# A two-layer decoder on one core: layer 0's first units in another order and its norm pinned behind the exps; in layer 1's joint attention the scaling one step later, copies bound to an engine, norms and routing in smaller pieces

## The chip, the cores and the metric

The kernel runs on one core of a Trainium2 chip. The metric is the device time of one launch in microseconds; it is compared by medians of several runs on the same chip. Beside the times there is one execution recorded by the hardware profiler. Engines are named as in the profile: PE is TensorE (matmuls and transposes; PEld its weight loads), DVE is VectorE, ACT is ScalarE, POOL is GpSimd, SP is the engine that only issues DMAs.

## The reference, cut to what matters

Input x has 8 batches of 512 tokens of 256 numbers, the context 64 tokens per batch. Everything is float32. `norm` is a layer norm without weights.

```python
# layer 0
x = norm(x + decay_attention(x))    # 16 heads of 16: softmax((q k^T / 16) * exp(-0.01 |i-j|)) v, k and v from a latent of 64
x = norm(x + cross_attention(x, context, mask))
x = norm(x + butterfly_ffn(x))      # its weight products are built on the chip, on POOL, during decay_attention
# layer 1
x = norm(x + causal_attention(x))   # 16 heads of 64, rotary positions
x = norm(x + joint_attention(x, context))   # 8 heads of 64; keys are 512 tokens + 64 of the context
xn = layernorm(x) * gamma + beta    # experts: top 2 of 8
p  = softmax(xn @ router.T / 1.5);  w, idx = top_k(p, 2)
x = norm(2 * x + sum over the 2 experts of w * (silu(xn @ W1[e]) @ W2[e]))
```

The residual counts twice (the expert layer adds it and the decoder adds it again), which is why the kernel doubles x before it stores it as the start of the sum.

## The kernel before

The kernel is recorded as one program; a scheduler places each engine's instructions by the order in which they were recorded and by its own estimate of when their operands are there. Inside `tc.manual_schedule(engines={PE})` PE keeps the recorded order exactly; an instruction given to `tc.keep_in_program_order` keeps its place among the others of its engine. PSUM tiles come from three pools, "s" (scores), "t" (transposes) and "o" (products); a tile of a pool can only be written again when its last reader is done. `evac` copies a PSUM tile to SBUF, in turn on DVE (L108) and ACT (L110).

**Layer 0's self attention.** A unit is a batch b and a group g of four heads; there are 32. Per unit, four `l0_maxima` compute scores of 128 queries against all keys (s_sc, L423), and a fused DVE operation multiplies by the decay and takes the row maximum (scored, L428); DVE then subtracts it on the diagonal block (diag, L438). `l0_shift` works the maximum into q and has POOL make four products (kr, kf, qf, qr, L459), so that the transposed scores can be computed directly: `l0_probs(b, g, kt)` for one block kt of 128 keys writes two tiles s_st (L472, L475, and the diagonal block by a transpose, L477), and ACT turns each into pt by an exp (L481). `l0_values` multiplies by v (L492). A step of the loop is (b, g, kt): probabilities of this unit, values of the step before, maxima of the unit two later, then a piece of work for other batches (`later`: transposes and projections of batch b+1, output product of batch b-1). The last piece of the output calls `normed(..., on_act=True)`: DVE adds the residual (L541) and takes statistics (L213, L214, ve L215), POOL raises to the power -1/2 (rs, L216), DVE makes the bias (ve, L218) and ACT scales (x<-r,ve,rs, L221). POOL's remaining time in this stage goes to the butterfly's weights (L299).

Ahead of the loop both first units are projected, all their 8 maxima computed, the first shifted, and the third projected. PE's order in layer 0 is the scheduler's.

**Layer 1's joint attention.** A step is (b, c, i): a pair of heads c, a block i of 128 queries; 128 steps. `_pipeline` runs, for step s, the scores of s (s_sc, L1106; DVE takes nm, L1110; ACT the exp, L1111; DVE the reciprocal of the sums, L900, and two scalings p<-p,rsum, L902), the transposes of step s-2 (tP2 L1123, tP L1128, evacuated by `evac`), the values of s-6 (o_pv, L1140 and L1148), a piece of projection for the next pair (`l1x_ahead`: t_qk L1060, t_v L1073), and one piece of the list `put_off`. That list gets, when a batch's values are done, its output product in two pieces (o_out, L239; the second ends with the norm), and then the routing: `route_norm` (z = norm of x, x doubled at L1196 and stored by SP), `route_transposes` (tZ, L1206, two PSUM tiles, copied by ACT with gamma and beta), `route_odds` (o_r, L1221, softmax), `route_picks` (the two largest; the token's number is copied into z, L1259), `route_places` (o_rank, ranks, and eight indirect DMAs from POOL that write rows of z to DRAM, L1283). z has a single buffer, so the next batch's writes into it wait for these DMAs. PE keeps the recorded order here.

**The experts** run over tiles of 128 or 256 routed rows: SP loads xr and the weights (L1406 to L1408), PE transposes and multiplies (L1418, L1440, L1457). The last batch's routing pieces are taken one per expert step from `last_route`.

Of the kernel before, what the change touches and what calls it, by code (L numbers as in the profile page):

```python
# [49 lines left out]
def decoder_kernel(ctx: ExitStack, tc: tile.TileContext, a: dict, out: bass.AP):  # L50
# [154 lines left out]

    def normed(dst, r, on_act=False):
# [9 lines left out]
        pool.tensor_tensor(rs, ve, mhalf, ALU.pow)  # L216
        if on_act:
            dve.scalar_tensor_tensor(ve, mv[:, :, 0], -1.0, rs, ALU.mult, ALU.mult)  # L218
        for i in range(NT):
            if on_act:  # L220
                act.activation(dst[:, i, :], r[:, i, :], AF.Identity, bias=ve[:, i : i + 1], scale=rs[:, i : i + 1])  # L221
                continue
            dve.tensor_scalar(
                dst[:, i, :], r[:, i, :], mv[:, i, 0:1], rs[:, i : i + 1], ALU.subtract, ALU.mult
            )

    def r_tile():
        return work.tile([P, NT, D], F32, tag="r", name="r", bufs=1)

    def project_and_norm(b, lhs, w, n, plus, later=None):  # L230

        r = r_tile()

        def piece(i2):
            o = u_tile("o_out").rearrange("p (i n) -> p i n", i=2)
            for j in range(2):
                i = 2 * i2 + j
                for c in range(n):
                    pe.matmul(  # L239
                        o[:, j, :],  # L240
                        lhsT=lhs[:, c, i * P : (i + 1) * P],
                        rhs=w[:, c, :],
                        start=(c == 0),
                        stop=(c == n - 1),
                    )
            dve.tensor_tensor(r[:, 2 * i2 : 2 * i2 + 2, :], o, plus[:, 2 * i2 : 2 * i2 + 2, :], ALU.add)
            if i2 == NT // 2 - 1:
                normed(xs[b], r)
# [214 lines left out]
    def l0_probs(b, g, kt):  # L463
# [15 lines left out]
        for s in s2:  # L479
            pt = ph.tile([P, 2, S], F32, tag="pt", name="pt", bufs=3)  # L480
            act.activation(pt, s, AF.Exp, scale=1.0 / 16.0)  # L481
            pts.append(pt)
# [39 lines left out]
    def l0_output(b):  # L522
# [10 lines left out]
        def product(i2):  # L533
# [8 lines left out]
            if i2 == 1:  # L542
                normed(xs[b], r, on_act=True)

        return [partial(turn, 0), partial(turn, 1), partial(product, 0), partial(product, 1)]

    with tc.tile_pool(name="bfly", bufs=1, side="right") as bfly, phase("l0_self") as ph, psum("a", 3, 1, 1):
# [8 lines left out]
        diags = [slot(f"diag{i}").rearrange("p (i h n) -> p i h n", i=NT, h=4) for i in range(2)]  # L556
        dve.tensor_tensor(wkT, wkT, wvT, ALU.add)
        o = o_tile("o_wlat")
        for c in range(KC):
            for k in range(KC):  # L560
                pe.matmul(
                    o[:, c * 64 : (c + 1) * 64],
                    lhsT=wkT[:, k, c * P : (c + 1) * P],
                    rhs=wdown[:, k, :],
                    start=(k == 0),
                    stop=(k == KC - 1),
                )
        dve.tensor_copy(wlat.rearrange("p c n -> p (c n)"), o[:, 0 : KC * 64])
# [4 lines left out]
        later = []  # L573
        for piece in l0_prepare(0):
            piece()
        for u in units[:2]:
            l0_project(*u)
        for u in units[:2]:
            for i in range(NT):
                l0_maxima(*u, i)  # L580
            if u == units[0]:
                l0_shift(*u)
        l0_project(*units[2])
        for n, (b, g) in enumerate(units):
            ahead2 = units[n + 2] if n + 2 < len(units) else None
            if g == 0 and b + 1 < NB:
                later.extend(l0_prepare(b + 1))
            for kt in range(NT):
# [4 lines left out]
                elif n:  # L593
                    l0_values(*units[n - 1], NT - 1)
                if ahead2:
                    l0_maxima(*ahead2, kt)

                if kt == 1:
                    if n + 1 < len(units):
                        l0_shift(*units[n + 1])  # L600
                elif kt == 2:
# [14 lines left out]
        for piece in later:  # L616
            piece()
        for _ in butterfly:
            pass
# [284 lines left out]
    put_off = []  # L904

    def groups(stage):

# [53 lines left out]
    def out_done(b, c, o, w, n, plus, then=None):  # L961
# [4 lines left out]
        if c == n - 1:  # L966
            project_and_norm(b, aT, w, n, plus(), put_off)
            if then:
                then(b)
# [126 lines left out]
    def l1x_scores(b, c, i):  # L1096
# [12 lines left out]
        for j, s in enumerate(ss):  # L1109
            dve.tensor_reduce(nm[:, j : j + 1], s, AX.XY, ALU.max, negate=True)  # L1110
            act.activation(  # L1111
                p[:, j, :].rearrange("p (t n) -> p t n", t=2), s, AF.Exp, bias=nm[:, j : j + 1], accum_out=sums[:, j : j + 1]
            )
        scaled(p, sums, S + S2)
        live["p", b, c, i] = p

    def l1x_transposes(b, c, i):
        p = live.pop(("p", b, c, i)).rearrange("p j n -> p (j n)")
        if i == 0:
# [3 lines left out]
        pe.transpose(t, p[:, S : S + P], ident)  # L1123
        evac(pt2[:, i * P : (i + 1) * P], t)
        for j in range(2):
            t = t_tile("tP")
            for k in range(NT):
                pe.transpose(t[:, k, :], p[:, (S + P) * j + k * P : (S + P) * j + (k + 1) * P], ident)  # L1128
            evac(pt[j][:, :, i * P : (i + 1) * P], t)

# [58 lines left out]
    def over_i(c):  # L1189
        return c.unsqueeze(1).to_broadcast([P, NT, NE])  # L1190

    def route_norm(b):
# [5 lines left out]
        live["z", b] = z  # L1198

# [37 lines left out]
    def greatest(pick, left):  # L1237
# [7 lines left out]
        return pick  # L1245

    def route_picks(b):
        pr = live.pop(("pr", b))
        rest = e_tile("rest")
        picks = [greatest(e_tile("pick0"), pr)]  # L1250
        dve.scalar_tensor_tensor(rest, picks[0], -2.0, pr, ALU.mult, ALU.add)
# [369 lines left out]
```

## Time and profile before

| | |
|---|---|
| median of 3 runs | 3543.11 us (3541.12 to 3548.39) |
| the profiled execution | 3548.88 us, its span 3547.2 us, mean granted clock of PE 0.965 |
| busy in the span: PE, DVE, ACT, POOL | 3332.7, 2082.5, 1510.1, 1115.3 us |

By stage, from the profile's windows:

| stage, us of the span | length | PE busy | DVE busy | ACT busy | POOL busy | PE clock |
|---|---|---|---|---|---|---|
| 0 to 62, loads and first units | 62 | 49.25 | 30.16 | 7.44 | 16.64 | 0.81 |
| 100 to 800, layer 0's self attention | 700 | 655.17 | 488.67 | 312.10 | 532.75 | 0.96 |
| 850 to 1260, cross attention and butterfly | 410 | 390.15 | 256.41 | 150.81 | 70.53 | 0.95 |
| 1260 to 2175, layer 1's causal attention | 915 | 882.19 | 645.10 | 518.64 | 224.22 | 0.99 |
| 2175 to 2985, joint attention | 810 | 757.38 | 535.29 | 340.88 | 100.75 | 0.97 |
| 2985 to 3502, experts | 517 | 513.08 | 70.01 | 120.57 | 115.69 | 1.00 |

A line such as `PE s_sc L423 <- ACT pt L481: 23.2, 6, 3.9` says that PE's instruction on line 423 stood idle for 23.2 us in total, 6 times, at most 3.9 us, until ACT's instruction on line 481 was done. In a timeline the columns are start, duration, engine, line, operation, output<-inputs, shapes and count; in square brackets is the engine's idle time ahead of it, and what ended that. A row of the windows has the stretch and its length, then for each of PE, PEld, DVE, ACT and POOL the busy time, then PE's granted clock, the DMA engines' share and GB/s.

### The profile page before, as it was taken

The numbers are of one execution on the slowest core, as the hardware profiler recorded it, in microseconds if no ns is written. First come the engines' busy times: TensorE is split into PE (matmuls) and PEld (weight loads), VectorE is DVE, ScalarE is ACT, GpSimd is POOL, SyncE is SP. The second block draws the span as 40 slices with busy tenths as digits, with TensorE's granted clock in tenths as the row PEclk, the third lists the DMA queues.
The fourth block names the chain that finished last, engine by engine and source line by source line (L and its number), as shares of the span: only waits on it lengthen the run. The fifth ranks groups of instructions, "written<-read, shape, count | busy, mean of one in ns | idle before, by whom it ended". The sixth has DMA issues, their size and how long they took to land. (4 is left out here: it accounts for less than half of the span.)

```text
span 3547.2 us, 52530 instructions
## 1 busy us (share of the span) xinstructions
PE 3332.7 (94%) x19574; PEld 2092.0 (59%) x19574; DVE 2082.5 (59%) x5710; ACT 1510.1 (43%) x3139; POOL 1115.3 (31%) x1032
## 2 busy tenths in 40 slices
PE   8989999998999989999999999999999998999995
PEld 3333434345666656666666666555555555888884
DVE  5777766675666556777777775666666665211012
ACT  2444444443443335655556654444444433222222
POOL 3868677772221122222222220011111111222222
PEclk8999999999999999999999999999999999999997
DMA  4100011111000079422333330000000004666674
GB/s 132 31 19 25 22 37 37 36 36 47 5 2 1 1 195 259 77 37 38 38 40 43 40 52 4 4 19 19 22 16 14 17 13 143 206 185 187 183 230 139
DMA packets 166001, 234.96 MB, mean 66 GB/s; under 512 B 26569, under 2 KB 128649, under 8 KB 165746
## 3 DMA queue, kind: packets, MB, share of 16 engines
q1 hardware_dynamic: 139010, 175.83, 15.8%
q0 software_dynamic: 25584, 51.57, 10.2%
q10 hardware_dynamic: 1152, 4.19, 0.3%
q8 instruction: 156, 2.56, 0.3%
q14 instruction: 99, 0.81, 0.1%
HBM read 135.83 MB, written 61.11 MB: 56 GB/s over the span
## 5 line engine op out<-in xcount | busy, mean ns | idle before, releaser
L428 DVE CUSTOM_DVE_ANT_0 scored<-s_sc,decay 128x512 f32<-128x512 f32 x512 | 323.5, 687 | 223.9 <-PE s_sc L423 222.7
L281 ACT ACTIVATE p<-p,nm 128x128 f32<-128x128 f32 (+3 forms) x512 | 282.5, 553 | 301.7 <-DVE nm L270 300.4
L865 POOL DMA_DIRECT2D qk<-turned x256 | 208.2, 1232 | 593.4 <-issue 304.6
L481 ACT ACTIVATE pt<-s_st 128x1024 f32<-128x1024 f32 x256 | 261.1, 1023 | 268.2 <-PE s_st L477 237.9
L902 DVE TENSOR_SCALAR p<-p,rsum 128x576 f32<-128x576 f32 (+4 forms) x768 | 300.3, 433 | 10.0
L1111 ACT ACTIVATE p<-s_sc,nm 128x576 f32<-128x576 f32 x256 | 189.6, 743 | 221.7 <-DVE nm L1110 200.8
L1477 DVE TENSOR_SCALAR y<-o_y,share 128x256 f32<-128x256 f32 x71 | 34.2, 483 | 408.9 <-PE o_y L1457 408.9
L1440 PE MATMUL s_h<-xnT,we 128*128 128x256 f32 (+1 forms) x1248 | 260.3, 362 | 0.0
L270 DVE CUSTOM_DVE_ANT_0 p<-s_sc,tabs 128x128 f32<-128x128 f32 (+3 forms) x512 | 225.1, 484 | 57.4 <-PE s_sc L925 57.3
L1457 PE MATMUL o_y<-we,h 128*128 128x256 f32 x1136 | 251.4, 379 | 0.0
L1457 PEld LDWEIGHTS o_y<-we,h 128*128 128x128 f32 x1136 | 215.3, 190 | 29.0
L1478 POOL DMA_INDIRECT total<-y,to x71 | 110.2, 1552 | 388.4 <-DVE y L1477 219.8
L1440 PEld LDWEIGHTS s_h<-xnT,we 128*128 128x128 f32 x1248 | 216.7, 191 | 24.3 <-ACT xnT L1419 0.2
L1110 DVE TENSOR_REDUCE nm<-s_sc 128x1 f32<-128x576 f32 x256 | 183.3, 748 | 72.7 <-PE s_sc L1106 71.7
L423 PE MATMUL s_sc<-k,q 32*128 32x512 f32 x1024 | 175.6, 674 | 25.8 <-ACT pt L481 23.2
L110 ACT COPY pt<-tP 128x512 f32<-128x512 f32 (+1 forms) x224 | 109.9, 491 | 208.5 <-PE tP L1123 117.7
L958 ACT COPY pt<-tP 128x384 f32<-128x384 f32 (+1 forms) x384 | 173.0, 514 | 45.3 <-PE tP L957 44.8
L925 PE MATMUL s_sc<-qk 64*128 64x128 f32 (+3 forms) x1024 | 176.8, 461 | 13.7 <-DMA qk<-turned 10.3
L1106 PE MATMUL s_sc<-k,q 64*128 64x288 f32 x1024 | 169.4, 440 | 7.7 <-ACT p L1111 7.5
L957 PE MATMUL tP<-ident,p 128*128 128x128 f32 x1280 | 169.5, 276 | 5.3 <-ACT pt L958 4.0
L957 PEld LDWEIGHTS tP<-ident,p 128*128 128x128 f32 x1280 | 144.9, 141 | 49.4 <-issue 28.0
L981 PE MATMUL o_pv<-pt,vc 128*64 128x128 f32 (+1 forms) x2304 | 167.5, 290 | 0.0
(280 smaller groups left out, 6474.0 us busy)
## 6 DMA issues: line engine op xcount, KB each, us to landing
we<-in_mo_w SPq DMA_DIRECT2D x78, 1024.0 KB, 5.5
rows_in<-zero SPq DMA_DIRECT2D x64, 530.0 KB, 13.2
qk<-turned POOLq DMA_DIRECT2D x256, 128.0 KB, 4.5
coef<-in_ff_upw SPq DMA_DIRECT2D x40, 256.0 KB, 3.3
coef<-in_ff_dnw SPq DMA_DIRECT2D x40, 256.0 KB, 3.2
xr<-rows_in SPq DMA_DIRECT2D x32, 265.0 KB, 5.7
x<-in_x SPq DMA_DIRECT2D x8, 512.0 KB, 9.9
total<-x SPq DMA_DIRECT2D x8, 512.0 KB, 2.9
```

What stands on the lines that cost most here:

```text
L270: dve.tensor_tensor_reduce(out=p[:, j, 0:n], in0=s[:, j, 0:n], in1=m, scale=-scale, scalar=3.0e38, op0=ALU.add, op1=ALU.min, accum_out=nm[ ...
L281: act.activation(p[:, j, 0:n], p[:, j, 0:n], AF.Exp, bias=nm[:, j : j + 1], scale=-1.0, accum_out=sums[:, at + j : at + j + 1],)
L428: dve.tensor_tensor_reduce(out=scored[:, h, :], in0=s[:, j, :], in1=decay[:, i, :], scale=1.0, scalar=-3.0e38, op0=ALU.mult, op1=ALU.max, ...
L481: act.activation(pt, s, AF.Exp, scale=1.0 / 16.0)
L865: pool.dma_start(out=qk[h : h + 32], in_=other[g : g + 32], accum_op=ALU.add)
L902: dve.tensor_scalar(p[:, j, 0:n], p[:, j, 0:n], rsum[:, j : j + 1], None, ALU.mult)
L925: pe.matmul(s[:, j, at : at + n], lhsT=q[h : h + 64, i * P : (i + 1) * P], rhs=k[h : h + 64, 0:n], start=True, stop=True,)
L957: pe.transpose(t[:, n, :], p[:, j, at * P : (at + 1) * P], ident)
L1110: dve.tensor_reduce(nm[:, j : j + 1], s, AX.XY, ALU.max, negate=True)
L1111: act.activation(p[:, j, :].rearrange("p (t n) -> p t n", t=2), s, AF.Exp, bias=nm[:, j : j + 1], accum_out=sums[:, j : j + 1])
L1440: pe.matmul(s[:, j, :], lhsT=w1[:, c, f * P : (f + 1) * P], rhs=xnT[:, c, :], start=(c == 0), stop=(c == KC - 1),)
L1457: pe.matmul(o, lhsT=h[:, f, i * P : (i + 1) * P], rhs=w2[:, f, :], start=(f == 0), stop=(f == 7),)
```

## The change

In layer 0:

- `normed` can hand its scaling back in a list (`then`) instead of recording it at once. Layer 0's output norm does so, and the main loop records the scaling at kt = 1, after that step's exps; the scalings and the exps are kept in program order on ACT.
- The start is written out in PE's own order: both transposes of x, then o_wlat, o_lat, the projection of unit 0, its maxima with the values' product and the projection of unit 1 between them, the shift, the projection of unit 2, and only two of unit 1's four maxima. The other two are taken in unit 0's steps, whose maxima go 2, 2, 1, 1.

In layer 1's joint attention:

- `l1x_scaled` (reciprocal and two scalings) is a stage of its own, recorded one step after its scores.
- The tP2 tile is always copied by ACT, tP's first by ACT and its second by DVE.
- The norms are taken apart: the output's norm statistics come with the second product, x's scaling one step later; z's statistics one step later, its scaling another one later; the doubling of x is moved to the step of tZ; the choice of experts is three pieces (`route_pick`, `route_picks`, `route_places`). The list is so 3 steps longer for most batches; for batch 6 two pairs of pieces are put together, and its list is one step longer than before. `last_route` has no empty pieces now.

```diff
-        for i in range(NT):
+        def scaling(held=lambda instruction: instruction):
             if on_act:
...
+        if then is None:
+            scaling()
+        else:
+            then.append(scaling)
...
-            act.activation(pt, s, AF.Exp, scale=1.0 / 16.0)
+            tc.keep_in_program_order(act.activation(pt, s, AF.Exp, scale=1.0 / 16.0))
...
-                normed(xs[b], r, on_act=True)
+                normed(xs[b], r, on_act=True, then=scalings)
...
-        for piece in l0_prepare(0):
-            piece()
-        for u in units[:2]:
-            l0_project(*u)
-        for u in units[:2]:
+        with tc.manual_schedule(engines={PE}):
+            turn0, turn1, latent, values = l0_prepare(0)
+            turn0()
+            turn1()
...
+            latent()
+            l0_project(*units[0])
+
+            between = [values, partial(l0_project, *units[1])]
             for i in range(NT):
-                l0_maxima(*u, i)
-            if u == units[0]:
-                l0_shift(*u)
-        l0_project(*units[2])
+                l0_maxima(*units[0], i)
+                if between:
+                    between.pop(0)()
+            l0_shift(*units[0])
+            l0_project(*units[2])
+
+            for i in range(2):
+                l0_maxima(*units[1], i)
         for n, (b, g) in enumerate(units):
-            ahead2 = units[n + 2] if n + 2 < len(units) else None
+
+            maxima = [(*units[n + 2], i) for i in range(NT)] if n + 2 < len(units) else []
+            if n == 0:
+                maxima = [(*units[1], i) for i in range(2, NT)] + maxima
...
-                if ahead2:
-                    l0_maxima(*ahead2, kt)
-
+                for _ in range(-(-len(maxima) // (NT - kt))):
+                    l0_maxima(*maxima.pop(0))
+
+                if kt == 1 and n + 1 < len(units):
+                    l0_shift(*units[n + 1])
                 if kt == 1:
-                    if n + 1 < len(units):
-                        l0_shift(*units[n + 1])
+
+                    if scalings:
+                        scalings.pop(0)(tc.keep_in_program_order)
...
-            project_and_norm(b, aT, w, n, plus(), put_off)
+            project_and_norm(b, aT, w, n, plus(), put_off, then_scaled)
...
-        scaled(p, sums, S + S2)
-        live["p", b, c, i] = p
+        live["p", b, c, i] = p, sums
+
+    def l1x_scaled(b, c, i):
+        p, sums = live["p", b, c, i]
+        scaled(p, sums, S + S2)
...
-        evac(pt2[:, i * P : (i + 1) * P], t)
+        act.copy(pt2[:, i * P : (i + 1) * P], t)
...
-            evac(pt[j][:, :, i * P : (i + 1) * P], t)
+            (act.copy, dve.tensor_copy)[j](pt[j][:, :, i * P : (i + 1) * P], t)
...
+    def route_scale(b):
+        then_scaled.pop(0)(tc.keep_in_program_order)
+
     def route_norm(b):
         z = keep.tile([P, NT, ROW], F32, tag="zr", name="z")
-        normed(z[:, :, 0:D], xs[b])
+        normed(z[:, :, 0:D], xs[b], then=then_scaled)
+        live["z", b] = z
+
+    def route_twice(b):
...
-        pieces = [partial(f, b) for f in (route_norm, route_transposes, route_odds, route_picks, route_places)]
+        pieces = [
+            route_scale,
+            route_norm,
+            route_scale,
+            both(route_transposes, route_twice),
+            route_odds,
+            route_pick,
+            route_picks,
+            route_places,
+        ]
+        if b == NB - 2:
+
+            pieces[0:2] = [both(*pieces[0:2])]
+            pieces[4:6] = [both(*pieces[4:6])]
+        pieces = [partial(f, b) for f in pieces]
         if b == NB - 1:
 
-            last_route.extend(pieces[:1] + 2 * [nothing] + pieces[1:])
+            last_route.extend(pieces)
             return
-
-        product = put_off.pop()
-        put_off.extend([lambda: (product(), pieces[0]()), nothing] + pieces[1:])
+        put_off.extend(pieces)
...
-            [(0, l1x_scores), (2, l1x_transposes), (6, l1x_values), (0, l1x_ahead)],
+            [(0, l1x_scores), (2, l1x_transposes), (1, l1x_scaled), (6, l1x_values), (0, l1x_ahead)],
```

In the order of the built programs, PE's instructions in the causal attention, the cross attention and the butterfly stand as before; of layer 0's self attention only the start of PE's order differs, and on ACT the place of the norm's four activations. The copy of the token's number into z (L1259 before) stands on DVE behind the evacuation and ahead of the reciprocal and scaling of the step, three steps later than before, as does o_rank of the batch before it.

More of the change, by code (lines that the diff above doesn't have):

```diff
@@ L204, in x_transposed, with normed @@
         return xT
-    def normed(dst, r, on_act=False):
+    def normed(dst, r, on_act=False, then=None):
         st = work.tile([P, NT, 6], F32, tag="st", name="st")
@@ L216, in normed, with project_and_norm @@
         pool.tensor_tensor(rs, ve, mhalf, ALU.pow)
-        if on_act:
-            dve.scalar_tensor_tensor(ve, mv[:, :, 0], -1.0, rs, ALU.mult, ALU.mult)
-        for i in range(NT):
+        def scaling(held=lambda instruction: instruction):
             if on_act:
[L221 to L225, printed above, removed]
+                dve.scalar_tensor_tensor(ve, mv[:, :, 0], -1.0, rs, ALU.mult, ALU.mult)
+            for i in range(NT):
+                if on_act:
+                    held(
+                        act.activation(dst[:, i, :], r[:, i, :], AF.Identity, bias=ve[:, i : i + 1], scale=rs[:, i : i + 1])
+                    )
+                    continue
+                held(
+                    dve.tensor_scalar(
+                        dst[:, i, :], r[:, i, :], mv[:, i, 0:1], rs[:, i : i + 1], ALU.subtract, ALU.mult
+                    )
+                )
+        if then is None:
+            scaling()
+        else:
+            then.append(scaling)
     def r_tile():
         return work.tile([P, NT, D], F32, tag="r", name="r", bufs=1)
-    def project_and_norm(b, lhs, w, n, plus, later=None):
+    def project_and_norm(b, lhs, w, n, plus, later=None, then=None):
         r = r_tile()
@@ L247, in piece @@
             if i2 == NT // 2 - 1:
-                normed(xs[b], r)
+                normed(xs[b], r, then=then)
         for i2 in range(NT // 2):
@@ L556, in decoder_kernel @@
         diags = [slot(f"diag{i}").rearrange("p (i h n) -> p i h n", i=NT, h=4) for i in range(2)]
[L557 to L568, printed above, removed]
         bias_row = bfly.tile([1, 1024], F32, name="bias_row")
@@ L572, in decoder_kernel @@
         units = [(b, g) for b in range(NB) for g in range(4)]
-        later = []
-        for piece in l0_prepare(0):
-            piece()
-        for u in units[:2]:
-            l0_project(*u)
-        for u in units[:2]:
-            for i in range(NT):
-                l0_maxima(*u, i)
-            if u == units[0]:
-                l0_shift(*u)
-        l0_project(*units[2])
+        later, scalings = [], []
+        with tc.manual_schedule(engines={PE}):
+            turn0, turn1, latent, values = l0_prepare(0)
+            turn0()
+            turn1()
+            dve.tensor_tensor(wkT, wkT, wvT, ALU.add)
+            o = o_tile("o_wlat")
+            for c in range(KC):
+                for k in range(KC):
+                    pe.matmul(
+                        o[:, c * 64 : (c + 1) * 64],
+                        lhsT=wkT[:, k, c * P : (c + 1) * P],
+                        rhs=wdown[:, k, :],
+                        start=(k == 0),
+                        stop=(k == KC - 1),
+                    )
+            dve.tensor_copy(wlat.rearrange("p c n -> p (c n)"), o[:, 0 : KC * 64])
+            latent()
+            l0_project(*units[0])
+            between = [values, partial(l0_project, *units[1])]
+            for i in range(NT):
+                l0_maxima(*units[0], i)
[5 more added lines that the diff above has]
+                l0_maxima(*units[1], i)
         for n, (b, g) in enumerate(units):
-            ahead2 = units[n + 2] if n + 2 < len(units) else None
+            maxima = [(*units[n + 2], i) for i in range(NT)] if n + 2 < len(units) else []
+            if n == 0:
+                maxima = [(*units[1], i) for i in range(2, NT)] + maxima
             if g == 0 and b + 1 < NB:
@@ L617, in decoder_kernel @@
             piece()
+        for scaling in scalings:
+            scaling()
         for _ in butterfly:
@@ L904, in decoder_kernel @@
     put_off = []
+    then_scaled = None
     def groups(stage):
@@ L1113, in l1x_scores @@
             )
+        live["p", b, c, i] = p, sums
+    def l1x_scaled(b, c, i):
+        p, sums = live["p", b, c, i]
         scaled(p, sums, S + S2)
-        live["p", b, c, i] = p
     def l1x_transposes(b, c, i):
-        p = live.pop(("p", b, c, i)).rearrange("p j n -> p (j n)")
+        p = live.pop(("p", b, c, i))[0].rearrange("p j n -> p (j n)")
         if i == 0:
@@ L1190, in over_i @@
         return c.unsqueeze(1).to_broadcast([P, NT, NE])
+    then_scaled = []
+    def route_scale(b):
+        then_scaled.pop(0)(tc.keep_in_program_order)
     def route_norm(b):
         z = keep.tile([P, NT, ROW], F32, tag="zr", name="z")
-        normed(z[:, :, 0:D], xs[b])
+        normed(z[:, :, 0:D], xs[b], then=then_scaled)
+        live["z", b] = z
+    def route_twice(b):
         dve.tensor_scalar(xs[b], xs[b], 2.0, None, ALU.mult)
         sp.dma_start(out=total[b * S : (b + 1) * S, :].rearrange("(i p) d -> p i d", p=P), in_=xs[b])
-        live["z", b] = z
     def route_transposes(b):
@@ L1245, in greatest, with route_pick @@
         return pick
+    def route_pick(b):
+        live["pick", b] = [greatest(e_tile("pick0"), live["pr", b])]
     def route_picks(b):
-        pr = live.pop(("pr", b))
+        pr, picks = live.pop(("pr", b)), live.pop(("pick", b))
         rest = e_tile("rest")
-        picks = [greatest(e_tile("pick0"), pr)]
         dve.scalar_tensor_tensor(rest, picks[0], -2.0, pr, ALU.mult, ALU.add)
@@ L1489, in routed, with both @@
     def routed(b):
-        pieces = [partial(f, b) for f in (route_norm, route_transposes, route_odds, route_picks, route_places)]
+        def both(f, g):
+            return lambda b: (f(b), g(b))
+        pieces = [
[12 more added lines that the diff above has]
+        pieces = [partial(f, b) for f in pieces]
         if b == NB - 1:
-            last_route.extend(pieces[:1] + 2 * [nothing] + pieces[1:])
+            last_route.extend(pieces)
             return
-        product = put_off.pop()
-        put_off.extend([lambda: (product(), pieces[0]()), nothing] + pieces[1:])
+        put_off.extend(pieces)
         if b == NB - 2:
```

## The prediction

> **What bounds the kernel now.** I read the page first: who is busy, and where its share or its clock drops.
>
> ```profile
> span 3547.2 us, 52530 instructions
> PE 3332.7 (94%) x19574; PEld 2092.0 (59%) x19574; DVE 2082.5 (59%) x5710; ACT 1510.1 (43%) x3139; POOL 1115.3 (31%) x1032
> PE   8989999998999989999999999999999998999995
> PEclk8999999999999999999999999999999999999997
> ```
>
> TensorE is the bound. The change leaves its instructions as they are in number and kind, so there are only two things to win: its idle time (3547.2 - 3332.7 = 214.5 us, some of it the start and the last 45 us) and the intervals at half clock behind idle stretches. Next the waits, first of PE, then of those that PE waits for:
>
> ```profile
> PE s_sc L423 <- ACT pt L481: 23.2, 6, 3.9
> PE tZ L1206 <- DVE pt L108: 17.0, 7, 2.8
> PE s_sc L1106 <- ACT p L1111: 7.5, 6, 2.8
> PE o_pv L1140 <- DVE aT L108: 5.8, 1, 5.8
> ...
> ACT x L221 <- DVE ve L218: 33.7, 7, 5.0
> ...
> DVE rsum L900 <- ACT p L1111: 55.5, 104, 1.0
> DVE z L1259 <- DMA rows_in<-z,irow: 44.1, 7, 7.1
> ```
>
> Six times, at the first step of batches 2 to 7, layer 0's scores wait 3.9 us for an exp. The exp isn't slow; it stands behind the scaling of an earlier batch's norm on ScalarE. The timelines of VectorE, ScalarE and TensorE at one of these, and the window around it:
>
> ```profile
> 250.94 1.23 DVE L218 SCALAR_TENSOR_TENSOR ve<-mv,rs 128x4 f32<-128x4 f32 x1 [1.15 <-POOL rs L216]
> 252.10 0.68 DVE L428 CUSTOM_DVE_ANT_0 scored<-s_sc,decay 128x512 f32<-128x512 f32 x1
> ...
> 252.21 2.08 ACT L221 ACTIVATE x<-r,ve,rs 128x256 f32<-128x256 f32 x4 [5.02 <-DVE ve L218]
> 254.19 1.91 ACT L481 ACTIVATE pt<-s_st 128x1024 f32<-128x1024 f32 x2
> ...
> 255.25 2.08 PE L423 MATMUL s_sc<-k,q 32*128 32x512 f32 x4 [3.90 <-ACT pt L481]
> ...
> 250.00:260.00 10.00, 6.11 (x33) 2.57 (x30) 4.46 (x10) 4.95 (x8) 7.08 (x6) 0.68 0.10 29
> ```
>
> ScalarE is idle for 5.02 us with finished s_st tiles behind it; TensorE idles 3.90 us and then runs slow (4 matmuls in 2.08 us, 1.13 before the gap; granted clock 0.68).
>
> **The change part by part.**
>
> *Layer 0, the norm pinned.* The four activations x<-r,ve,rs move from ahead of the exps of a batch's first step (group 0, kt 0) to behind those of kt 1, seven times. Measured by distance between the first diag transposes of neighbouring steps, kt 0 of the six slow batches takes 9.9 to 11.3 us (others 4.98) and kt 1 takes 5.2 to 6.5 (4.97): together 42 us. What stays: VectorE's order is unchanged, so it still waits for POOL's rs and issues ve, and its first maxima start at 252.10 and end about 253.4, while TensorE could enter kt 1 at about 252.4. So 1 us, say 1.2, is left per boundary, 7 us in all. The 2.08 us of activations land between the exps of kt 1 and kt 2; two exps take 1.91 and a step 4.97, so they fit (3.99). At the seventh place, group 2 of batch 7, ScalarE already ends a wait (2.7 us), +1. Gain 42 - 7 - 1 = 34.
>
> *Layer 0, the start.* The first scores are masked by VectorE from 30.30 on, after 16.39 us of idle; the first s_st comes at
>
> ```profile
> 60.80 0.93 PE L475 MATMUL s_st<-qf,kr 32*128 32x384 f32 x8
> ```
>
> since all 32 head pairs of two units are done first. After, unit 0's scores need only tT, o_wlat, o_lat and one s_qk. The transposes fill part of PE's first 8.16 us; the copy of wlat falls behind VectorE's decay tables (13.9 us), +1. First maximum about 26.3, first s_st about 48. But six maxima of unit 1 and 2 per 4 steps remain: the first two steps hold two each (2 x 3.4 us of VectorE, from 30.30 to 33.70 for one, against 4.97). Unit 1 so starts about 74.5 instead of 82.8. Gain 8, between 4 and 13.
>
> *Layer 1, the scaling a step later.* VectorE's 55.5 us of waiting for exps goes; it is idle time of an engine that isn't the bound, gain 0. The cost: now p is scaled about 6.7 us before its transposes; after, nm (1.42), the evacuation (0.68) and rsum (0.17) of the next step stand ahead of the two scalings (0.95), and about 1.9 us are left, 1.0 after the shorter steps (4.32 us instead of 5.23). 3.2 us of work in 5.23, 3.9 with a k copy: I take 0 in ordinary steps; the other end is the slow rival below.
>
> *Copies by place.* 64 evacuations of 128x128 leave VectorE (0.28 each, 17.9 in all) for ScalarE, which has 340 busy us in 810. Cover: ScalarE's idle time. Without it 0.3 per step.
>
> *Norms and routing in more pieces.* Now the norm, the z norm and the doubling of x stand together in one step, and tZ waits: (b,2,0) takes 9.3 us, about 3.1 too many, with 1 to 2 more at the half clock behind and 0.9 at (2,3): 32 us over seven batches. After, four smaller bits: x's scaling and the z scaling each come ahead of a scaling that transposes await. I take 1.2 at (2,0), 0.1 at (2,1), 1.6 at (2,3), where tZ's two banks are held until ScalarE has copied them after its exps, so that the step's transposes and t_v follow each other through one bank, and 0.5 behind: 3.4 for six batches, 3.5 for batch 6, 24 in all. Gain 8.
>
> The copy of token numbers into z (L1259) waits for the eight indirect DMAs that read that buffer's rows, 5.8 to 7.1 us each time, with everything on VectorE behind it:
>
> ```profile
> 2356.74 0.17 DVE L1259 COPY z<-tokens_at 128x4 f32<-128x4 f32 x1 [5.83 <-DMA rows_in<-z,irow]
> ...
> 2359.35 3.51 PE L1060 MATMUL t_qk<-xT,q_k 128*128 128x512 f32 x4 [3.64 <-DVE pt L108]
> ```
>
> This costs 34 us over six batches. The change moves o_rank and places three steps later and the copy equally, behind the evacuation but ahead of rsum and the scaling that is now only a step early. POOL's queue keeps its eight scatters in the same order. I take 6.6 instead of 5.7 each: -5. The doubled x's store on SP moves with its piece and nothing waits for it.
>
> *Ends of the stage.* At the start about 2 of gain. At its end VectorE's stall of 6.75 no longer stands ahead of aT(7,2), on which the 5.8 us wait of PE rests (with half clock 7). But batch 6's list comes a step later, and SP issues xr, then we, behind it; I put that wait at 3 to 4. Gain 3, from -2 to +7. Of the last batch the list comes one expert later (about 14 us), its block is used last.
>
> [...] Trace: behind a gap of only 1.60 us TensorE was granted 0.57.
>
> ```profile
> 2668.56 2.07 PE L1106 MATMUL s_sc<-k,q 64*128 64x288 f32 x8 [1.60 <-ACT p L1111]
> ...
> 2670.00:2674.00 4.00, 4.00 (x17) 2.13 (x14) 3.12 (x7) 2.28 (x6) 0.00 (x0) 0.57 0.00 0
> ```
>
> [...] Trace:
>
> ```profile
> 193.43 9.27 DVE L438 TENSOR_TENSOR diag<-scored,mx 128x512 f32<-128x512 f32 x1
> ```
>
> It outlasted seven POOL operations of 1.25 in a row; its median is 0.82. It happened twice (5.9 and 6.6 us for PE). [...] Kept at two, 0 to 4: ±12.
>
> **Sum.** 34 + 8 + 0 + 8 - 5 + 2 + 3 = 50. The profiled execution took 3548.88 (span 3547.2), 5.8 above the median, so 3548.9 - 50 = 3498.9, and for the median 3543.1 - 50 = 3493. About 0.2% (7 us) is what a measurement of this kernel can tell from no change.
>
> **The rivals.**
> - *The boundary only swaps its waiter.* VectorE stands until 252.10 for ve and POOL's 1.03 us power; if that or the longer ScalarE queue at kt 2 leaves 3.9 of gaps with half clock behind, 17 of the 34 go: 3510. For it: ve itself took 1.23 instead of the 0.17 of the operation of its shape before it (L215). Against: one s_st tile's wait is about 1 us by the times above.
> - *The context loses instead of gaining.* The one-bank step, the clock at 1.6 us gaps and the z stall one scaling closer: -8 becomes +12: 3513. For it: the row at 2668.56. Against: PE has four groups of work in between.
> - *Slower: the scaling becomes the last wait of each step.* Place: tP of each of the 128 steps of layer 1's context; price: whatever exceeds the 1.9 us (1.0 in a fourth of the steps). It decides from 50 / 128 = 0.39 us per step; at 0.55 it costs 70 and gives 3563. [...] Against: VectorE is 535 us busy in these 810, and loses 18 of them.
> - *More is won:* the aT stall goes whole, the boundaries close wholly, no 9 us lock falls into layer 0: 3475.
>
> **How the numbers follow.** My sum 0.50 (its own range 3480 to 3508), swapped waiter 0.12, context loses 0.14, more 0.11: faster 0.87. Half-way to the slow rival, within 0.2%: 0.04. The slow rival 0.09. The range 3474 to 3531 leaves out the last two and a few in a hundred at the low end.
>
> **What would show it.** Right: the first s_st near 48; no s_sc of layer 0 waiting for pt; x not waiting for ve; clock 1.00 in the slices of layer 0; tZ no longer waiting 2.8 us; z<-tokens_at still waiting some 40 us. Wrong: tP waiting for p by VectorE in most context steps; s_st waiting for mx more than the 19.3 us of now; diag rows of 9 us in number; the experts' first tZ waiting over 5 us.

## The result and the profile after

The changed kernel takes 3518.05 us in the median of 4 runs (3515.31 to 3523.69), before on the same chip 3545.32 us (3541.12 to 3548.39); the ratio is 0.9936, interval 0.9915 to 0.9956, so 15 to 30 us faster; the medians are 27 us apart. The profiled executions are 3548.88 us before and 3516.91 us after, 32.0 us apart: that of before is its slowest, that of after near its fastest. The forecast was 50. The steps below are read from the profiled executions, spans 3547.2 and 3514.8 us. Over the four occasions on which it was measured, before itself had medians of 3545 to 3556 us, so other kernels are compared by their ratio.

The page of after, the lines that answer to those shown of before:

```profile
span 3514.8 us, 52601 instructions
PE 3316.0 (94%) x19574; PEld 2088.9 (59%) x19574; DVE 2069.4 (59%) x5646; ACT 1526.0 (43%) x3203; POOL 1115.6 (32%) x1032
PE   7999999998999989999999999999999999999995
PEclk8999999998999999999999999999999999999997
```

Its waits (engine, line, waited for: us in total, times, longest), of PE, of DVE, and of ACT within the joint attention:

```profile
PE tP L1159 <- DVE k L1094: 31.1, 6, 5.6
PE s_st L483 <- DVE mx L439: 23.1, 48, 3.9
PE o_r L1259 <- ACT xnT L1245: 6.9, 12, 0.9
PE tP L1159 <- ACT pt L1160: 5.8, 6, 1.0
PE tM L465 <- DVE mneg L460: 5.3, 1, 5.3
...
DVE rsum L926 <- ACT p L1139: 78.8, 94, 1.0
DVE z L1299 <- DMA rows_in<-z,irow: 47.8, 7, 7.4
...
ACT xnT L1245 <- PE t_v L1101: 18.0, 6, 3.0
```

The six waits of s_sc for pt (23.2 us) and the seven of tZ (17.0) are gone. New ones stand in their place: six of tP behind a DVE copy, tM at the start, and o_r and tP around ACT's xnT. DVE's wait for the exps, expected to vanish, grew from 55.5 to 78.8.

In the table a stage's length is the distance between matmuls in the trace: in layer 0 the first diag transposes of (b, g, kt), in the joint attention the first s_sc of (b, c, i).

| stretch | before | after | gained | forecast |
|---|---|---|---|---|
| start, to unit 1's first diag transposes | 82.83 | 86.39 | -3.6 | +8 |
| rest of layer 0's self attention, to (7,3,3) | 743.05 | 701.25 | 41.8 | 34 |
| cross attention, butterfly, causal attention | 1348.27 | 1347.93 | 0.3 | 0 |
| joint attention, (0,0,0) to (7,3,3) | 785.01 | 797.44 | -12.4 | +5 |
| from there to the end | 588.04 | 581.79 | 6.3 | +3 |

The stretches sum to 32.4 us. The third is the same instructions in both; over the kernels below it varied from 1344 to 1352, so differences of a few us in a whole span say little, and single steps are compared instead. The joint attention varies too: five kernels with the same instructions there (after, e_startback, e_pool, e_fill128, e_fill32) took 797.44 to 809.25 us.

Step by step, the joint attention's -12.4 us is -9.3 where VectorE stands behind the eight scatters (the indirect DMAs; called the scatters' stall below), -4.4 in the routing's steps, (b,2,0) to (b,3,2), and +1.3 elsewhere.

The boundary that the prediction showed, in after (ACT, then PE, then the window around it):

```profile
248.42 1.02 ACT L492 ACTIVATE pt<-s_st 128x1024 f32<-128x1024 f32 x1 [1.99 <-PE s_st L488]
249.63 1.02 ACT L492 ACTIVATE pt<-s_st 128x1024 f32<-128x1024 f32 x1 [0.19 <-PE o_pv L503]
...
252.71 0.38 PE L483 MATMUL s_st<-qr,kf 32*128 32x128 f32 x2 [1.07 <-DVE mx L439]
...
250.00:260.00 10.00, 8.76 (x80) 4.14 (x72) 9.13 (x20) 6.65 (x10) 7.27 (x7) 1.00 0.13 29
```

The exps start as soon as s_st is there. PE has one gap of 1.07 us, for the maxima that DVE starts late because it still waits for rs, and the clock stays at 1.00. The step takes 5.67 us, was 11.25.

At the start PE waits 5.25 us for mneg, the clock is at half (0.50) from 34.6 to 65.3 us, and the first two steps of the loop, from 53.85 and from 63.38 us, take 9.5 and 9.7 us. The first runs at half clock, the second mostly at full; in both DVE waits about 3 us for scores (windows of after, then DVE):

```profile
34.00:66.00 32.00, 26.64 (x90) 10.96 (x94) 18.36 (x49) 4.73 (x7) 8.72 (x7) 0.52 0.10 37
...
53.85:63.38 9.53, 9.53 (x43) 4.76 (x41) 6.46 (x19) 2.52 (x3) 0.00 (x0) 0.50 0.00 0
...
65.30:72.10 6.80, 5.47 (x40) 1.96 (x34) 4.93 (x14) 1.02 (x1) 0.00 (x0) 1.00 0.00 0
...
57.02 0.69 DVE L439 CUSTOM_DVE_ANT_0 scored<-s_sc,decay 128x512 f32<-128x512 f32 x1 [2.86 <-PE s_sc L434]
...
67.00 0.69 DVE L439 CUSTOM_DVE_ANT_0 scored<-s_sc,decay 128x512 f32<-128x512 f32 x1 [3.22 <-PE s_sc L434]
```

Two timelines carry what was lost in the joint attention. Step (2,0,3), DVE and PE:

```profile
2332.61 0.19 DVE L1299 COPY z<-tokens_at 128x4 f32<-128x4 f32 x1 [7.36 <-DMA rows_in<-z,irow]
...
2333.76 0.68 DVE L1094 COPY k<-t_qk 128x512 f32<-128x512 f32 x1
...
2334.51 1.11 PE L1159 MATMUL tP<-ident,p 128*128 128x128 f32 x4 [5.64 <-DVE k L1094]
```

and step (1,2,3), ACT and PE, with the window behind it:

```profile
2286.28 1.45 ACT L1245 ACTIVATE xnT<-tZ,gb 128x512 f32<-128x512 f32 x2 [3.00 <-PE t_v L1101]
...
2282.60 0.66 PE L1159 MATMUL tP<-ident,p 128*128 128x128 f32 x4 [0.97 <-ACT pt L1160]
...
2287.11 0.39 PE L1259 MATMUL o_r<-rw,xnT 128*128 128x8 f32 x2 [0.87 <-ACT xnT L1245]
...
2290.00:2294.00 4.00, 4.00 (x19) 2.16 (x15) 3.35 (x12) 2.53 (x7) 0.00 (x0) 0.60 0.00 0
```

ACT has nothing to do for 3.00 us although tZ was transposed at 2278.15 to 2279.19. It waits for t_v, a matmul that has nothing to do with tZ. What they share is a buffer, as the third experiment shows.

### The profile page after: what moved, and what is told of

It reads as the page before. It is cut to its first block, busy times and chain, and to the rows that moved or that the text cites. A ratio compares the mean times of both kernels' runs of the same rounds, so it can differ in the third digit from the quotient of the medians.

```text
span 3514.8 us, 52601 instructions
## 1 busy us (share of the span) xinstructions
PE 3316.0 (94%) x19574; PEld 2088.9 (59%) x19574; DVE 2069.4 (59%) x5646; ACT 1526.0 (43%) x3203; POOL 1115.6 (32%) x1032
## 5 line engine op out<-in xcount | busy, mean ns | idle before, releaser
L1159 PE MATMUL tP<-ident,p 128*128 128x128 f32 x1024 | 143.9, 284 | 39.1 <-DVE k L1094 31.1
L985 PE MATMUL tP<-ident,p 128*128 128x128 f32 x1280 | 169.4, 276 | 5.8 <-ACT pt L986 4.5
L985 PEld LDWEIGHTS tP<-ident,p 128*128 128x128 f32 x1280 | 144.4, 141 | 49.7 <-issue 27.9
L449 DVE TENSOR_TENSOR diag<-scored,mx 128x512 f32<-128x512 f32 x128 | 163.0, 1274 | 2.4
```

The costliest lines, as they stand in the source:

```text
L985: pe.transpose(t[:, n, :], p[:, j, at * P : (at + 1) * P], ident)
```

## The experiments

"(b,2,3)" is a step of the joint attention unless layer 0 is named. The joint attention's length is that of the table above; spans are those of the profiled executions.

| kernel | span | median | ratio to before (interval) | joint attention |
|---|---|---|---|---|
| after | 3514.8 | 3518.05 | 0.9936 (0.9915 to 0.9956) | 797.44 |
| e_pinonly | 3512.3 | 3507.21 | 0.9876 (0.9858 to 0.9894) | 788.68 |
| e_startback | 3519.7 | 3521.78 | 0.9912 (0.9891 to 0.9933) | 801.23 |
| e_xnr | 3491.5 | 3496.95 | 0.9854 (0.9838 to 0.9871) | 776.05 |
| e_zpin | 3480.7 | 3477.82 | 0.9789 (0.9771 to 0.9808) | 754.00 |
| best1 | 3441.4 | 3442.47 | 0.968 (0.9664 to 0.9696) | 725.38 |
| e_pinz | 3469.2 | 3469.23 | 0.9755 (0.9738 to 0.9771) | 753.25 |
| e_lagback | 3534.4 | 3529.7 | 0.9919 (0.9903 to 0.9936) | 803.70 |
| e_piecesback | 3518.4 | 3513.54 | 0.9875 (0.9859 to 0.9892) | 788.40 |
| e_copyback | 3521.3 | 3526.03 | 0.9926 (0.99 to 0.9951) | 806.27 |
| e_pool | 3518.4 | 3523.18 | 0.9918 (0.9895 to 0.9941) | 799.69 |

**The norm's pin alone**, in before:

```diff
-            act.activation(pt, s, AF.Exp, scale=1.0 / 16.0)
+            tc.keep_in_program_order(act.activation(pt, s, AF.Exp, scale=1.0 / 16.0))
...
+                    if scalings:
+                        scalings.pop(0)(tc.keep_in_program_order)
```

> Before with one part of the change alone: layer 0's norm handed back and its four activations and the exps pinned on ACT. Theory (from the two traces' steps): the six boundary steps fall from 9.9 to 11.3 us to about 5.65 and step (7,2,1) from 6.46 to about 3.0, so the profiled span falls by 36 to 44 us against 3547.2, to about 3507, and nothing moves elsewhere. That alone would be faster than the whole change (3514.8). Rival: the start of after is needed for part of it, and the gain is under 30.

The span falls by 34.9 us, a little under the range expected. The boundary steps are 5.63 to 5.67 us and (7,2,1) of layer 0 is 3.03, as expected. By its ratio the one edit is at least as good as the whole change: 0.9876 against 0.9936, with intervals that don't touch. Everything else in the change together gained nothing that shows (spans 3512.3 and 3514.8).

**The start put back**, in after (before's start, its PE order left to the scheduler).

> After with before's start of layer 0 put back. Theory: the new start costs, because PE waits 5.25 us for mneg and then runs 30.7 us at half clock: the span falls by 3.6 us from 3514.8 to about 3511, and the first diag transpose comes later again (61.7 instead of 53.9) with unit 1 at 82.8. Rival (the prediction's sum): the new start is worth 8 us, so this span rises to about 3523.

Unit 1's first transposes come at 80.88 instead of 86.39, although the first diag comes 5.9 us later. But these arrivals vary with the start unchanged: before's start has unit 1 at 80.88 to 84.13 in four kernels, the new one at 82.76 to 88.12 in seven. On average the new start is 2.4 us later, and the ranges overlap. So it is shown that the start did not gain 8 us; that it costs, as the theory had it, is likely but not shown. The whole span rose by 4.9, not fell by 3.6: layer 0 gave back 2.7, since a 9.27 us diag stood at unit (1,2) again, as in before, and the other stages varied.

**xnT in a buffer of its own**, in after:

```diff
-        xnT = work.tile([P, KC, S], F32, tag="xT", name="xnT")
+        xnT = r_tile().rearrange("p i d -> p (i d)").rearrange("p (c n) -> p c n", c=KC)
```

> After with xnT put into the buffer of r (free in those steps) instead of one of the two buffers that it shares with xT. Theory: at (2,3) ACT's copies of tZ wait for t_v, the last reader of the old xT, whose buffer xnT has to take since tZ now comes after the next batch's xT; tZ's two PSUM tiles are held so long. With its own place the copies come right behind the exps or before; step (2,3) falls from 10.33 to 7.0 or 7.5, (3,0) from 6.86 to 5.23: 4 to 5 us in each of six batches, the span falls by 24 to 30 to about 3488. Rival (the prediction): tZ's tiles are held by ACT's exps, and the buffer makes no difference: under 5 us in all.

Step (b,2,3) is 6.98 in all six batches (10.33), (b,3,0) 5.23 (6.80 to 6.86). ACT now goes with tZ, not with t_v:

```profile
2274.81 1.45 ACT L1245 ACTIVATE r<-tZ,gb 128x512 f32<-128x512 f32 x2 [1.19 <-PE tZ L1244]
```

This shows the cause. xT has two buffers, and xnT takes one of them. Before the change tZ came ahead of the next batch's xT, and a buffer was free. Now tZ is recorded one step behind it, so xnT gets the buffer of the xT whose last reader is t_v in (b,2,3). Until then ACT can't empty tZ's two PSUM tiles, and the step's transposes share the third. The price is 3.35 + 1.6 us in each of six batches, 30 us; the span fell by 23.3, and 21.4 are seen in the stage, since the six steps with the scatters' stall were 7.3 us longer in this run (tP behind k: 35.2 instead of 31.1).

**The token copy kept in program order**, in after:

```diff
-        dve.tensor_copy(z[:, :, D + NE], tokens_at[:, b * NT : (b + 1) * NT])
+        tc.keep_in_program_order(dve.tensor_copy(z[:, :, D + NE], tokens_at[:, b * NT : (b + 1) * NT]))
```

> After with the copy of the token numbers into z (L1299) kept in program order on DVE, so behind the choice of experts, 32 steps later, long after the eight scatters that it waits for. Theory: the waits of DVE on rows_in (47.8 us, 7 times) and of tP on DVE k (31.1 us) go, step (b,0,3) falls from about 12.6 to 5.29 six times: 43.8 us; the span falls to about 3471. Rival: z's norm scaling, which writes the same buffer, takes over the wait, or half clock stays for another reason: less than half of it.

Step (b,0,3) is 5.29 in all six batches, the joint attention 43.4 us shorter, and the two waits are gone:

```profile
PE s_st L483 <- DVE mx L439: 26.7, 48, 4.0
PE s_q L882 <- DVE nm L281: 12.2, 7, 2.9
```

are the first lines of PE's waits now. (In "32 steps later" the expectation miscounts; the copy moves from (b,0,3) to the step of the choice of experts, 10 steps on.) The span fell by 34.1: the rest of layer 0, with one long diag more, took 6.7 back, the start 1.7 (unit 1 at 88.12), the end 4.6.

**All three edits together, with unit 2's projection ahead of unit 0's shift:**

> After with three edits together: xnT in r's buffer, the token copy kept in program order, and at the start the projection of unit 2 ahead of unit 0's shift, so that it fills PE's 5.25 us wait for mneg. Theory: 43.8 us and 26 us add up (different steps, both seen alone), and the start no longer falls to half clock so early: first steps 9.5 and 9.7 fall to about 7, some 4 to 8 us. Span 3514.8 - 44 - 25 - 6 = about 3440. Rival: with the z stall gone, the next wait takes its place (ACT's xnT, or the scaling one step late), and the sum falls short by 15 or more; the start stays at half clock, since the gap only moves.

Joint attention 725.38, 72 us less than after; in its window PE is busy for 720.18 of 725.40 at full clock:

```profile
2134.00:2859.40 725.40, 720.18 (x4021) 421.77 (x4020) 513.02 (x1229) 353.22 (x865) 95.95 (x138) 1.00 0.05 16
```

No new wait took the place of the old ones. Unit 1 came at 82.67, but e_xnr, with after's start, had it at 82.76, so no gain of the third edit is shown. The first two steps still take 9.52 and 9.37 us, the first at half clock (its 16 matmuls of s_sc take 5.57 us; 8 take 1.14 earlier, at 30.43): the rival was right there. At 0.968 this version is faster than both kernels.

**Before with the pin and the token copy alone:**

> Before with only two edits: layer 0's norm pinned, and the token copy kept in program order; layer 1's scaling, copies and routing pieces as before. It tells whether the context part of the change is worth anything once its two losses are known. Theory: 35 from the pin and 34 from the stall, span about 3547 - 69 = 3478; the routing's own losses (9.3 at (b,2,0) and half clock behind, some 30 us) stay, so that the three-edit version of after is faster by 30 or more. Rival: the pieces are worth nothing and the two are within 10 us.

753.25 in the joint attention, with (b,2,0) still 9.3 to 10.0. Against best1 the pieces, places and lag are worth 27.9 us, once what they brought along is taken away (30 or more were expected).

**The scaling back to lag 0**, in after:

> After with the scaling of p back in the step of its scores (lag 0), everything else of the change kept. Theory (prediction): the lag itself is worth nothing in ordinary steps: 5.23, 4.32 and 5.29 stay to the hundredth, and the span moves by less than 8 us. Rival 1: it is what lets the norms pass (VectorE not waiting for exps with the norm behind it), then (b,2,0) or (b,2,1) grow by 1 us or more per batch, some 10 us slower. Rival 2: the lag hurts at the z stall, where only one step lies between the scaling and the transposes; without it (b,0,3) falls from 12.6 to 9 or less, some 20 us faster.

The ordinary steps are the same within 0.03 us, and so are (b,2,0) and, in six batches of seven, (b,2,1); neither rival shows. The stage is 6.3 us longer, in the stalled steps (3,0,3), (6,0,3) and (7,0,3) and at (5,3,0), and the span longer by more, with a long diag in layer 0; that is no more than the same instructions vary by. The reason for the indifference is in the timeline of after's ordinary step (DVE, ACT):

```profile
2342.56 0.68 DVE L1160 COPY pt<-tP 128x512 f32<-128x512 f32 x1
2344.15 0.17 DVE L926 RECIPROCAL rsum<-sums 128x2 f32<-128x2 f32 x1 [0.91 <-ACT p L1139]
...
2343.27 0.75 ACT L1139 ACTIVATE p<-s_sc,nm 128x576 f32<-128x576 f32 x1
```

rsum waits for the exp of its own step. The scaling is recorded a step later, but the scheduler issues it in the old place. The one-step lag hardly exists on the engine.

**The routing's pieces put back**, in after:

> After with the norms and the routing in before's five pieces, scaling lag and copies by place kept. Theory: tZ comes ahead of the next batch's xT again, so xnT has a free buffer: (2,3) and (3,0) lose nothing (5.0 per batch back), the z stall is that of before (34 instead of 44), but (b,2,0) takes over 9 us again with half clock behind (4.6 per batch lost): span about 3505. Rival: with the scaling a step later the long norm step delays the scalings that the next transposes need, and it is slower than after by 10 or more.

(b,2,3) 6.31, (b,3,0) 5.23, (b,2,0) 9.0 to 9.6 again. The stage is 9.0 us shorter than after's, about as expected, though the scatters' stall costs 6.7 us a batch where before's 5.7 was expected; it now shows as s_sc behind the exps:

```profile
PE s_sc L1134 <- ACT p L1139: 26.0, 14, 4.7
PE tZ L1239 <- DVE pt L1160: 15.4, 7, 2.2
```

The span, expected near 3505, is 3518.4, since the rest of layer 0 (one long diag more), the third stretch and the end took 14 us more than in after. In the change as it stands the smaller pieces lose about 9 us in the stage; with xnT's buffer cured (e_xnr, 776.05) they gain 12.

**The copies back to alternating:**

> After with the copies of tP2 and tP put back to the alternating evac, the rest kept. Theory (prediction): nothing, ordinary steps stay 5.23, 4.32, 5.29, the span moves less than 8 us. Rival: the fixed places pay in the crowded steps, where ACT has the first copy ahead of its exps: (b,2,3) or (b,0,3) grow by 1 us or more per batch, 6 to 15 us slower.

The rival: (b,2,0) is 6.87 to 6.90 in four batches (5.23), with a wait that after doesn't have, and (b,2,3) 11.1 to 13.7 in the same four (10.33), against 0.6 to 1.0 won at (b,2,1).

```profile
PE t_qk L1088 <- DVE pt L108: 6.3, 4, 1.6
```

The stage is 8.8 us longer, which alone would show nothing, since the same instructions vary by 12. But PE's waits in (b,2,0), (b,2,1) and (b,2,3) of batches 1 to 6 sum to 24.1 us, against 16.5 in each of the five kernels with after's joint attention. So the places are worth some 8 us of waiting here, where the prediction had nothing; the medians can't tell the two kernels apart.

**Work put into PE's gap at the start**, ten matmuls of 128 rows, or of 32 (the result is used by nothing; one execution of each, 3521.00 and 3531.77 us):

```diff
+            spare = t_tile("spare").rearrange("p i n -> p (i n)")
+            for _ in range(10):
+                pe.matmul(spare, lhsT=live["xT", 0][:, 0, 0:P], rhs=live["xT", 0][:, 0, :], start=True, stop=True)
             l0_shift(*units[0])
```

> After with ten matmuls of 128 rows by 512 columns (about 0.5 us each, result unused) ahead of unit 0's transposes tM, in PE's wait of 5.25 us for mneg at 33.7 us. Both theories of the slow start say that with the gap filled by such work the clock stays full at least until tM; the half-clock interval of 30.7 us shrinks to under 10, the first two steps fall from 9.5 and 9.7 to about 6.8, the first diag transpose from 53.9 to about 49, unit 1 from 86.4 to about 77. If it doesn't, the start's loss isn't the gap.

> The same ten matmuls with 32 rows instead of 128, so the same busy time of PE with a quarter of the array. Theory A (before lost its clock at 35.2 us in the middle of 32-row scores with gaps of 0.2 and 1.05 us only): matmuls of 32 rows don't hold the clock, half clock begins near 35 and the first steps take 9.5 as in after. Theory B (only busy time counts): the same result as with 128 rows.

The filling took longer than the gap (8.85 and 11.5 us, tM at 42.3 and 44.0 instead of 38.9), so the arrival times of the two are not to be compared with after's. The clock is. Windows inside the filling, of e_fill128 and of e_fill32, then e_fill128's first step of the loop with the start of the second:

```profile
37.30:42.30 5.00, 4.98 (x12) 1.90 (x10) 1.18 (x4) 0.00 (x0) 0.00 (x0) 1.00 0.01 3
...
37.30:43.90 6.60, 6.60 (x8) 2.01 (x7) 0.97 (x4) 0.00 (x0) 0.00 (x0) 0.50 0.01 2
...
53.70:65.70 12.00, 12.00 (x54) 5.67 (x52) 6.90 (x20) 3.55 (x4) 0.00 (x0) 0.52 0.00 0
```

With 128 rows the clock is full (1.00) through the gap, with 32 rows it is at half (0.50) in the middle of unbroken work: theory A. But filling the gap didn't save the steps: both take 9.5 and 9.7 again. A gap of 1.70 us waiting for the maxima came at 50.5, the four s_st behind it took 1.65 us where four ahead of it had taken 0.91, and then 12.00 us of unbroken work, mostly of 32 rows, ran at 0.52. The clock came back at 65.3, within the second step, which is no shorter for it. In after, 32-row matmuls are 87% of PE's matmul time in the first step; in later stretches of layer 0 they are 53 to 57%, and there the clock is 1.00 (300 to 320 us, 600 to 620 us). That their share holds the first step at half clock is so far argued: no run changed it.

**POOL's butterfly dealt otherwise**, `range((3, 1, 3, 3)[kt])` for `range(3 - kt % 2)`:

> After with POOL's butterfly operations dealt 3, 1, 3, 3 to the steps of a unit instead of 3, 2, 3, 2, so that fewer stand next to the four products of the shift at kt 1. Theory: the diag of 9.4 us at 410 (and that at 193 to 200 where it comes) is VectorE shut out by an unbroken row of POOL operations; with another dealing the row is broken there or somewhere else arises: one of the long diags more or less, 6 us each way. Rival: the long diags have nothing to do with POOL's row, and stay at the same units.

The diag at 413.0 is as long as ever (9.37), and the one at unit (1,2) came back (195.5, 9.29). They stay at their units, as the rival has it, but the edit didn't put the theory to the test: the row of POOL operations beside each is 14 long in this kernel as in after. DVE, then the first and the last operation of POOL's row:

```profile
413.03 9.37 DVE L449 TENSOR_TENSOR diag<-scored,mx 128x512 f32<-128x512 f32 x1
...
403.73 1.65 POOL L470 TENSOR_TENSOR qf<-q,w 128x512 f32<-128x512 f32 x1 [4.63 <-DVE q L466]
...
420.60 1.25 POOL L470 TENSOR_TENSOR kf<-k,w 128x512 f32<-128x512 f32 x1
```

The traces speak against the rival's reason. In the kernels of this document there are 23 diags of 9 us, and each ends 0.55 us after the end of POOL's row. But layer 0 of after has 30 unbroken rows of 8 us or more, all with a diag that begins inside, and in 29 of them it takes at most 3.3 us, mostly 1.5. So each long diag ends with its row; what decides that one becomes long remains open. Of the kernels with the new start five lack the one at (1,2) (after, e_xnr, e_copyback, e_fill128, e_fill32) and five have it (e_zpin, best1, e_lagback, e_piecesback, e_pool).

## What the prediction had right, and which steps failed

- **Bound and direction:** right. PE's idle time (214.5 us of the span before, 198.8 after) and half clock (mean granted clock 0.965 and 0.97) decide, the change is faster, 3518 lies in the range; but 27 us, not 50.
- **The pin of the norm:** right in mechanism and size. The boundaries gave 36.7 us where 35 was worked out (1.07 us of gap left; 1 to 1.2 predicted). (7,2,1) gave 3.4 where -1 was expected: there too a norm's scaling had stood ahead of the exps, and the wait of 2.73 us went with it. One of the two long diags fell away, and three half-clock intervals of 3.4 us stand there now (from 164, 328 and 727 us): +1.7, within the ±12. That range's 0 to 4 long diags were the author's estimate from before's two: all kernels with the pin have one or two.
- **The start, +8: the step that failed first.** Unit 1 came at 86.39, not 74.5. First maximum 22.9 (26.3 predicted), better than thought; first s_st 50.18 (48). The error is in "the first two steps hold two each (2 x 3.4 us of VectorE": they were costed by DVE at full clock of PE, 6.8 us. They took 9.52 and 9.66. VectorE's share was sized about right (6.46 us busy in the first), but it doesn't work without a break: it waits 2.86 and 3.22 us for PE's scores, and PE's s_st then wait for its maxima. The first step, moreover, ran at half clock (0.50), for which the sum has no term, though before's start shows it too (0.50 from 35 to 59). The second was at full clock for 6.80 of its 9.66 us, so the half clock alone isn't the cause. Filling the gap cured neither; what would is open. In e_fill128 the clock came back only after 13 us of unbroken work (52.2 to 65.3).
- **"1.6 at (2,3)": the step that failed most.** Where 1.6 and 0.5 behind were put down, it cost 3.35 there and 1.6 in the step behind, 5.0 per batch and 30 us in six. With a buffer of its own (e_xnr) PE has no wait in (b,2,3), and steps (b,2,0) to (b,3,2) of batches 1 to 6 take 243.7 us, against 265.4 before and 272.4 after: but for the buffer the pieces would have won more than the 8 forecast. That tZ's banks are held was seen; by what was not. The prediction named ACT's exps and missed that tZ moved behind the allocation of the next xT, whose buffers xnT shares. A moved step was costed by engines and PSUM, not by the SBUF buffer that it takes.
- **The clock at small gaps:** the sum lets the gaps that are left over cost nothing beyond their length. That was the author's estimate, which no run shows to hold in general, and before's row at 2668.56 (0.57 behind 1.60 us) spoke against it. At (2,3) the row was right: behind gaps of 0.36, 0.97, 0.87 and 0.28 us within 7 us the window shows 0.60. This is the 1.6 us at (b,3,0), in all six batches of after, though not in every kernel (batches 1 and 2 of e_startback lack it behind the same waits). At five boundaries the estimate was (1.03 to 1.07 us, the clock stays at 1.00); at the sixth, batch 7, a gap of 1.40 us was followed by half clock for 3.4 us, from 727.
- **The scatters' stall, 6.6 each:** 7.3 measured (43.8 in six batches, 34.5 before), so -9.3 for -5. Right in kind.
- **The scaling a step later:** "0 in ordinary steps" is right, for a wrong reason. It was argued that the lag leaves 1.9 us; in the trace the scaling isn't later. The 55.5 us of waits grew to 78.8. So the slow rival, whose place was the 1.9 us, could not come about.
- **Copies by place, 0:** some 8 us of PE's waits, by the run that undid them.
- **The end of the stage, +3:** 6.3, the high end of what these instructions gave (0.9 to 6.3 over the kernels with the new pieces). PE waits 0.89 us for aT instead of 5.85, and the experts' first transposes came without the 3 to 4 us wait that was set against it.

Of the rivals, "the context loses instead of gaining" (+12) is what happened there, -12.4 us, together with a start that no case had. That the number fits is in part luck: of its reasons the clock at small gaps and the stall came true, but the buffer, the largest, is not among them. The sum: 50 - 11.6 (start) + 7.8 (rest of layer 0) + 0.3 - 17.4 (joint attention) + 3.3 (end) = 32.4.

## What to carry to other kernels

When a step is moved in a program with tile pools, list the buffers that it takes as well as the engines: a tile that shares a tag inherits the wait for whoever read that buffer last, and the profile shows it as an engine waiting for an instruction that it has nothing to do with. An early-ready copy that a scheduler lets float forward can carry a long DMA wait to the head of a busy queue; keeping it in its recorded place was worth 43 us of the stage, more than the whole change. And after recording something "one step later", look at where it is issued.

## What the runs showed of the hardware

- In unbroken work on 32-row matmuls PE was granted 0.50 over 6.60 us (e_fill32), on 128-row ones in the same place 1.00 over 5.00 us (e_fill128; one execution each). And 12.00 us of unbroken work, 69% of its matmul time of 32 rows, ran at 0.52 (e_fill128), while later stretches of after with 53 to 57% ran at 1.00. What happens between them was not measured.
- In after a half-clock interval of 3.4 us followed on the gaps of 0.36, 0.97, 0.87 and 0.28 us at (b,2,3), in all six batches, on one of 1.10 us at 163, one of 1.40 us at 726 and one of 1.54 us at 2142; in before on the one of 1.60 us at 2668.56. Not on all: five gaps of 1.03 to 1.07 us in after had none behind them, and in e_copyback four steps (b,2,0) with gaps of 1.57 to 1.60 us grew by 1.64 to 1.67 us only.
- A VectorE operation with both inputs in SBUF (diag, before, at 193.43) took 9.27 us, where its median is 0.82: seven GpSimd operations of 1.25 us began after it in an unbroken row, and it ended 0.55 us after the last of them. In 29 of the 30 such rows of after the diags inside took 0.69 to 3.3 us. Why that one took longer was not shown.
